# A four-layer graph network in groups of eight graphs: the stages of a group put beside other groups' stages, roots as powers on GpSimd

## The chip, the cores and the metric

The kernel runs on one core of one Trainium2 chip. A core has five engines that run side by side, each with a queue of its own that it works off in order: TensorE (PE: matrix products, and PEld for its weight loads), VectorE (DVE), ScalarE (ACT), GpSimd (POOL) and SyncE (SP, which here issues DMAs). Data lies in SBUF (128 partitions) and in PSUM, where products land. ACT evaluates functions from tables; a set of functions has to be loaded before one of them can run.

The metric is the device time of one execution in microseconds (us). Times of single instructions come from one profiled execution.

## The reference

128 graphs of 64 nodes with 128 features and a 64x64 adjacency pass four layers. Every layer is `x = x + layer(relu(layernorm(x)), adj)`; only the parts that the change touches are written out.

```
# layer 0: over each edge (i, j), with e = adj[i, j]
g  = exp(coeff * (e - offsets)**2)                  # 64 gaussians
Wf = ssp(g @ W1.T + b1) @ W2.T + b2                 # ssp(x) = softplus(x) - log 2
y  = sum_j (h @ Wa.T)[j] * Wf[i, j] * e * e
x  = x + ssp(y @ Wd1.T + bd1) @ Wd2.T + bd2
# layer 1: hyperbolic attention
h  = proj(mobius_add(proj(mobius_matvec(W, h)), hyp_bias))   # norms, artanh, tanh
att[i, j] = sigmoid(silu(logmap(h_i, h_j) @ att_w1.T + att_b1) @ att_w2.T + att_b2)
s  = mlp(x_self, sum_j att * logmap(h_i, h_j) * adj) + x_self
o  = proj(expmap(s, h))                              # norm, tanh
x  = x + proj(expmap0(silu(logmap0(o))))             # norm, artanh, norm, tanh
# layer 2
x  = x + (D^-1/2 adj D^-1/2 h) @ W + b
# layer 3: deg = adj.sum over senders
m  = where(deg > 0, (adj.T @ (h @ Ws)) / max(deg, 1) + h @ Wr, 0)
x  = x + concat(h, m) @ W_upd
```

## The kernel before

`sparse_stack` works on 16 groups of 8 graphs; a tile of 128 partitions holds two graphs, and a group is four such pairs (`NP = 4`), so most tiles are 128x512. The kernel sorts each graph's nodes by degree and packs the edges of a row into slots: 12 items for a group, 8 of 512 slots and 4 of 275. (`dense_stack`, for inputs that don't fit the slots, isn't run.)

A group g passes five stages, each a Python generator that emits instructions and yields between steps:

- `order(g)` (L1144): sorts nodes, permutes x and adj, builds the slot masks `oh`, the first layer norm and `rf`. 9 steps.
- `layer0(g)` (L1228): for each item a spread of adj over nodes (L1260), Square and Exp, products with W1 and rf (L1275, L1277), Exp, copy and Ln on ACT, a product with W2 (L1286), and on DVE the multiplication and gather (L1288, L1113). At its end (L1334 to L1353) the gathered sums `ys` pass two small products with Exp and Ln between, and give `x1`. 56 steps.
- `layer1_nodes(g)` (L1380): what layer 1 needs for each node and pair of nodes: norms, artanh, tanh, Gram matrices, the tables `U`, `Sx`, `qn`, `mp`, `pq`. 26 steps.
- `layer1_edges(g)` (L1517), the slots of layer 1: for each item products (L1538, L1553, L1556), Silu on ACT, a product to scores (L1564), Tanh on ACT, and on DVE masking and gather. 55 steps.
- `rest(g)` (L1618): end of layer 1, layers 2 and 3, the store. 39 steps. It is a chain of short operations on tiles of one group.

The order of ACT's instructions is the order in which the program emits them (`manual_schedule`, L1798); PE's, DVE's and POOL's queues are ordered by a planner that looks at costs and dependences. `together` (L770) emits several stages in proportion to their steps; `abreast` (L783) takes a step of each in turn. The main loop (L1805 to L1812) runs two stretches for a group g, one after the other: `layer1_edges(g)` with `order(g + 2)`, then `layer0(g + 2)` with `rest(g)` and `layer1_nodes(g + 1)`.

The helper `act` (L999) puts a table load on ACT where the function asked for is in another set than the last: Exp and Ln are in one set, Silu and Tanh in another; Square, Copy and Relu need no load. Roots are Ln and then Exp with a factor (`root`, L1089; `moments`, L1053), so `rest`, which also has Silu and Tanh, changes sets several times, and it changes them for layer 0 too, whose Exp and Ln stand between in ACT's queue. `artanh_ratio` (L1077) is two Ln on ACT and a series on DVE.

POOL has three operations for a group: L1342, L1645, L1729, additions over 128x512. PSUM is full: three buffers `big` of two banks, one `sm`, one `sl`. The wide tiles of `rest` (d0 to d3) and of `layer1_nodes` (b0 to b3) are separate.

Of the kernel before, what the change touches and what calls it, by code (L numbers as in the profile page):

```python
# [11 lines left out]
F32 = mybir.dt.float32  # L12
# [8 lines left out]
NP = 4  # L21
# [744 lines left out]
STEPS0, STEPS1, ORDER, NODES1, REST = 56, 55, 9, 26, 39  # L766
# [3 lines left out]
def together(*gens):  # L770

    gens = [(g, n) for g, n in gens if g is not None]
    most = max(n for _, n in gens)
    for i in range(most):
        for g, n in gens:
            for _ in range((i + 1) * n // most - i * n // most):
                next(g, None)
    for g, _ in gens:
        for _ in g:
            pass  # L780
# [12 lines left out]
def sparse_stack(ctx: ExitStack, tc: tile.TileContext, ins, out: bass.AP, flag):  # L793
# [34 lines left out]
    epsc = const.tile([P, 1], F32, name="epsc")  # L828
    G.memset(epsc, EPS_LN)
# [49 lines left out]
    def weight_t(ap, name, dst=None):  # L879
# [3 lines left out]
        if dst is None:  # L883
# [72 lines left out]
    wmsg = const.tile([P, 2 * P], F32, name="wmsg")  # L956
    nc.sync.dma_start(out=wmsg.rearrange("d (s u) -> d s u", s=2),
                      in_=ins["L3_gnn_W_msg"].rearrange("(s d) u -> d s u", s=2))
    wupd = const.tile([P, 2, P], F32, name="wupd")
    nc.sync.dma_start(out=wupd, in_=ins["L3_gnn_W_upd"].rearrange("(s d) u -> d s u", s=2))  # L960

# [6 lines left out]
    state = {"evac": S, "set": None}  # L968
    HALF = [slice(0, N), slice(N, P)]

    def evac(dst, src):

        if state["evac"] is S:
            S.copy(dst, src)
        else:
            V.tensor_copy(dst, src)
# [75 lines left out]

    def moments(x):  # L1053

        raw, mv = ttile("ln_raw", NP, 6), ttile("ln_mv", NP, 2)
        bn(mv, raw, x)
        yield
        rstd = ttile("ln_r")
        act(AF.Ln, rstd, mv[:, :, 1], bias=epsc)
        act(AF.Exp, rstd, rstd, scale=-0.5)  # L1060
        return mv, rstd

# [26 lines left out]
    def root(n):  # L1089

        act(AF.Ln, n, n)
        act(AF.Exp, n, n, scale=0.5)
# [43 lines left out]
    def load(g):  # L1136
        x = pers.tile([P, NP, D], F32, name="x", tag="x")
        adj = pers.tile([P, NP, N], F32, name="adj", tag="adj", bufs=4)
        gs = slice(2 * NP * g, 2 * NP * (g + 1))
        nc.sync.dma_start(out=adj, in_=adj_d[gs].rearrange("(p b) i j -> (b i) p j", b=2))  # L1140
        nc.sync.dma_start(out=x, in_=x_d[gs].rearrange("(p b) i d -> (b i) p d", b=2))
        return {"x": x, "adj": adj}

    def order(g, st):  # L1144
# [19 lines left out]
        xp = st["xp"] = wtile("xp")  # L1164
# [10 lines left out]
        adjT = st["adjT"] = etile("adjT", 3)  # L1175
        raw, mv = ttile("ln_raw", NP, 6), tiny.tile([P, NP, 2], F32, name="mv0", tag="mv0")
        bn(mv, raw, xp)
        st["mv"] = mv
# [9 lines left out]
        V.tensor_tensor(h, xp, bl(mv[:, :, 0], D), ALU.subtract)  # L1188
        yield
        oh = st["oh"] = pers.tile([P, NP, SLOTS + SLOTS % 2], BF, name="oh", tag="oh", bufs=3)  # L1190
        for c in range(3):
# [9 lines left out]
            elif c == 1:  # L1201
                act(AF.Relu, hT, pt)
                pt = pairs_mm(hT, lambda p: waT)
            else:
                st["rf"] = wtile("a2")
                evac(st["rf"], pt)
# [21 lines left out]
    def layer0(st):  # L1228

        xp, oh, adjT, rf = st["xp"], st["oh"], st["adjT"], st["rf"]  # L1230
        sr = ttile("sr")
        act(AF.Ln, sr, st["mv"][:, :, 1], bias=epsc)
        act(AF.Exp, sr, sr, scale=-0.25)
        ys = [wtile(f"y{c}") for c in range(2)]
# [71 lines left out]
        for t in range(n + 1):  # L1306
# [20 lines left out]
            if t % 2 == 0:  # L1327
                if t + 2 < n:
                    squares((t + 2) // 2)
                if t + 4 < n:  # L1330
# [3 lines left out]
        spn = wtile("a0")  # L1334
        pt = big()
        pre, x1p = pt[:, 0, :], pt[:, 1, :]
        T.matmul(pre, lhsT=wd1T, rhs=flat(ys[0]), start=True, stop=False)
        T.matmul(pre, lhsT=wd1T, rhs=flat(ys[1]), start=False, stop=False)
        T.matmul(pre.rearrange("q (x r) -> q x r", r=N)[:, :, 0:RC], lhsT=wd1T, rhs=ys[2],
                 start=False, stop=True)  # L1340
        xb = wtile("a2")
        G.tensor_tensor(xb, xp, bm(bd2s, NP), ALU.add)  # L1342
        yield
        ex = wtile("a1")
        act(AF.Exp, flat(ex), pre, bias=bd1)
        V.tensor_scalar(ex, ex, EXP_MAX, None, ALU.min)
        act(AF.Ln, ex, ex, bias=1.0)
        V.scalar_tensor_tensor(flat(spn), pre, bd1, flat(ex), ALU.add, ALU.max)
        x1 = st["x1"] = pers.tile([P, NP, D], F32, name="x1", tag="x1", bufs=3)
        for p in range(NP):  # L1350
            T.matmul(x1p[:, D * p:D * p + D], lhsT=spn[:, p, :], rhs=wd2T, start=True, stop=True)
        V.tensor_tensor(flat(x1), x1p, flat(xb), ALU.add)
        yield  # L1353

# [14 lines left out]
    def proj_scale(v, tmp, hn, sc):  # L1369

        act(AF.Square, tmp, v)
        reduce_d(hn, tmp)
        V.tensor_scalar(hn, hn, MIN_NORM2, None, ALU.max)
        yield
        root(hn)
        V.reciprocal(sc, hn)
        V.tensor_scalar(sc, sc, MAXNORM, 1.0, ALU.mult, ALU.min)
        yield

    def layer1_nodes(st):  # L1380

        x1 = st["x1"]
        mv, rstd = yield from moments(x1)
        h1, tmp, hT = wtile("b0"), wtile("b1"), wtile("b2")
# [10 lines left out]
        mx = wtile("b3")  # L1395
# [7 lines left out]
        nn = ttile("nn", 2, NP)  # L1403
        V.tensor_scalar(nn, n2, MIN_NORM2, None, ALU.max)
        yield
        root(nn)
# [3 lines left out]
        yield  # L1410
        artanh_ratio(r, s)
        rr, arg = ttile("rr", 2, NP), ttile("arg")
        V.reciprocal(rr, nn)
        V.tensor_tensor(arg, r, s, ALU.mult)
        V.tensor_tensor(arg, arg, rr[:, 0], ALU.mult)
        V.tensor_tensor(arg, arg, mxn, ALU.mult)
        yield
        yield
        t = ttile("t")
        act(AF.Tanh, t, arg)  # L1420
# [8 lines left out]
        yield  # L1429
# [5 lines left out]
        yield from proj_scale(mx, tmp, hn, sc)  # L1435
# [81 lines left out]
    def layer1_edges(st):  # L1517
# [100 lines left out]
    def rest(g, st):  # L1618
# [8 lines left out]
        supT, xsT = wtile("d1"), wtile("d2")  # L1627
# [13 lines left out]
        hid = wtile("d0")  # L1641
# [7 lines left out]
        u, tmp, tmp2 = wtile("d3"), wtile("d1"), wtile("d2")  # L1649
# [3 lines left out]
        un2, un, uh, k_ = ttile("un2"), ttile("un"), ttile("uh"), ttile("k_")  # L1653
        act(AF.Square, tmp, u)
        V.tensor_tensor(tmp2, u, hh, ALU.mult)
        reduce_d(uh, tmp2)
        reduce_d(un2, tmp)
        V.tensor_scalar(un, un2, MIN_NORM2, None, ALU.max)
        rb = ttile("rb")
        V.tensor_scalar(rb, st["beta"], 1e-15, None, ALU.max)  # L1660
        V.reciprocal(rb, rb)
        yield
        root(un)
        V.tensor_tensor(rb, rb, un, ALU.mult)
        V.reciprocal(un, un)
# [3 lines left out]
        V.tensor_tensor(k_, k_, un, ALU.mult)  # L1669
# [7 lines left out]
        scaled(tmp, hh, ca)  # L1677
        scaled(u, u, cc)
        V.tensor_tensor(u, u, tmp, ALU.add)
        yield  # L1680
        hn, sc = ttile("d_hn"), ttile("d_sc")
        yield from proj_scale(u, tmp, hn, sc)

        s, r = ttile("d_s"), ttile("d_r")
        V.tensor_tensor(s, hn, sc, ALU.mult)
        V.tensor_scalar(s, s, ATMAX, 1e-15, ALU.min, ALU.max)
        yield
        artanh_ratio(r, s)
        V.tensor_tensor(r, r, sc, ALU.mult)
        scaled(u, u, r)  # L1690
        yield
        yield
        act(AF.Silu, u, u)
        act(AF.Square, tmp, u)
        reduce_d(un2, tmp)
        V.tensor_scalar(un, un2, MIN_NORM2, None, ALU.max)
        yield
        yield
        root(un)
# [3 lines left out]
        V.reciprocal(un, un)  # L1703
        V.tensor_tensor(k_, k_, un, ALU.mult)
        x2 = wtile("x2")
        scaled(u, u, k_)
        V.tensor_tensor(x2, u, x1, ALU.add)
        yield
# [9 lines left out]
        mv, rstd = yield from moments(x2)  # L1718
        act(AF.Ln, dn, dn)
        act(AF.Exp, dn, dn, scale=-0.5)  # L1720
        V.tensor_tensor(rstd, rstd, dn, ALU.mult)
        hs = wtile("d2")
        normed(hs, x2, mv, rstd)
        yield
        sT = wtile("d0")
# [5 lines left out]
        x3r = wtile("d3")  # L1731
        V.tensor_tensor(x3r, pairs_mm(sT, lambda p: w2g), bl(dn, D), ALU.mult)
        V.tensor_tensor(x3r, x3r, x2, ALU.add)
# [21 lines left out]
        V.tensor_scalar(ind, deg, 0.0, None, ALU.is_gt)  # L1755
        V.tensor_scalar(rdeg, deg, 1.0, None, ALU.max)
        V.reciprocal(rdeg, rdeg)
        V.tensor_tensor(rdeg, rdeg, ind, ALU.mult)
        mv, rstd = yield from moments(x3)
        h3, h3T = wtile("d2"), wtile("d1")  # L1760
        normed(h3, x3, mv, rstd)
        yield
        pt = transposes(h3)
# [3 lines left out]
        xs, xr = wtile("d0"), wtile("d3")  # L1767
        for q in range(NP // 2):
            pt = bank(2 * P)
            for k in range(2):  # L1770
                T.matmul(pt[:, k, :], lhsT=h3T[:, 2 * q + k, :], rhs=wmsg, start=True, stop=True)  # L1771
            yield
            two = slice(2 * q, 2 * q + 2)
            evac(xs[:, two, :], pt[:, :, 0:P])
            V.tensor_tensor(xr[:, two, :], pt[:, :, P:2 * P], bl(ind[:, two], D), ALU.mult)
        yield
        msg, msgT, y = wtile("d2"), wtile("x2"), wtile("d3")
        pt = bank()
        graphs_mm(pt, adj, xs)
        V.tensor_tensor(msg, pt, bl(rdeg, D), ALU.mult)  # L1780
# [68 lines left out]
```

## Time and profile before

| | us |
|---|---|
| median of 3 runs | 2774.13 (2764.31 to 2775.21) |
| the profiled execution | 2772.69 |
| its span, first to last instruction | 2770.9 |
| PE busy | 2244.2 (81%) |
| DVE busy | 2041.9 (74%) |
| ACT busy | 1714.9 (62%) |
| of it table loads, 189 of 1.283 us | 242.5 |
| POOL busy | 111.1 (4%) |
| mean granted clock of PE, share of full speed | 0.876 |

Times in the profile are from the span's start. A row of the windows view gives a stretch, its length, and for each engine its busy time and instructions in it, the granted clock of PE, the share of DMA and GB/s. A row of the timeline gives start, duration, engine, line, operation and tiles, and in brackets how long the engine had been idle and what ended that. A row of the groups by line gives a count, then the busy time of the group and the mean duration of one in ns, then idle time before them. Helpers give their own line to all their callers: L1009 is every function on ACT, L974 every copy out of PSUM on ACT, L1113 every gather, L1107 every spread, L1003 and L1007 the table loads. The chain that ended last is 46% PE, 36% ACT and 15% DVE of the span.

### The profile page before, as it was taken

The page shows a single profiled execution, that of the slowest core. Times are in us where ns is not written, and L with a number is a line of the kernel's source. Part 1 is how long each engine was busy: PE and PEld are TensorE (multiplying, and loading weights), DVE is VectorE, ACT ScalarE, POOL GpSimd, SP SyncE. Part 2 cuts the span into 40 slices and gives each one's busy share as a digit, 9 for nine tenths or more (in the row PEclk, how much of TensorE's full clock was granted, in tenths as well). Part 3 has the DMA queues.
Part 4 walks back from the last instruction along what each step waited for, and adds up shares of the span by engine and source line. Part 5 has one row for each costly group of instructions (what it writes and reads, how often), then busy time and mean ns, then how long its engine had stood idle before and what let it go on. Part 6 is the DMA issues. An engine that isn't in the chain of part 4 may idle for free.

```text
span 2770.9 us, 28227 instructions
## 1 busy us (share of the span) xinstructions
PE 2244.2 (81%) x9841; PEld 1067.9 (39%) x9841; DVE 2041.9 (74%) x4741; ACT 1714.9 (62%) x2769; POOL 111.1 (4%) x72
## 2 busy tenths in 40 slices
PE   5889797887979888797988979788797987979483
PEld 2433343434434343343434434343343434434232
DVE  4587877877777777877777787777877777776653
ACT  3676848476584856749375673846749376583432
POOL 0000000000000000000000000000000000000000
PEclk9889899998989989898898988989899898988585
DMA  1000000000000000000000000000000000000000
GB/s 38 4 4 1 0 10 0 10 1 2 8 1 10 1 6 4 1 10 1 10 1 6 5 1 10 0 6 4 1 10 0 7 0 1 5 0 4 1 4 6
DMA packets 29498, 13.72 MB, mean 5 GB/s; under 512 B 10528, under 2 KB 29344, under 8 KB 29344
## 3 DMA queue, kind: packets, MB, share of 16 engines
q1 hardware_dynamic: 29344, 11.80, 1.6%
q8 instruction: 80, 1.31, 0.2%
q14 instruction: 74, 0.61, 0.1%
HBM read 7.61 MB, written 4.19 MB: 4 GB/s over the span
## 4 chain that ended last, share of the span: by engine, by line
PE 46%; ACT 36%; DVE 15%; issue 2%; DMA 0%; SPq 0%; DVEq 0%; ACTq 0%
ACT ex L1009 8%; PE big L1553 6%; PE big L1286 6%; PE sl L1564 6%; PE big L1538 6%; ACT e L1009 5%; PE big L1556 5%; ACT L1003 4%; ACT L1007 3%; ACT va L1009 3%; ACT ra L1009 3%; PE sm L1029 3%; PE sl L1260 2%; PE sm L1771 2%; DVE ex L1288 2%
## 5 line engine op out<-in xcount | busy, mean ns | idle before, releaser
L1286 PE MATMUL big<-ex,w2T 128*128 128x512 f32 (+1 forms) x768 | 420.1, 680 | 104.3 <-ACT ex L1009 103.2
L1009 ACT ACTIVATE ex<-big,c_L_gnn_att_b 128x1024 f32<-128x1024 f32 (+1 forms) x192 | 188.5, 982 | 327.3 <-PE big L1556 327.3
L1260 PE MATMUL sl<-va,bones 128*128 128x512 f32 (+1 forms) x384 | 211.4, 637 | 94.6 <-ACT e L1009 75.3
L1288 DVE SCALAR_TENSOR_TENSOR ex<-big,c_L_gnn_b,ra 128x1024 f32<-128x1024 f32 x128 | 163.9, 1281 | 160.9 <-PE big L1286 145.4
L1286 PEld LDWEIGHTS big<-ex,w2T 128*128 128x128 f32 x768 | 163.4, 233 | 285.1 <-ACT ex L1009 160.4
L1275 PE MATMUL big<-e,w1T 64*128 64x512 f32 (+1 forms) x768 | 224.2, 621 | 59.9 <-ACT e L1009 43.0
L1277 PE MATMUL big<-va,a 64*128 64x512 f32 (+1 forms) x768 | 213.6, 578 | 27.0 <-ACT ex L1009 22.5
L1553 PE MATMUL big<-va,U 64*128 64x512 f32 (+1 forms) x768 | 216.4, 571 | 0.0
L1009 ACT ACTIVATE ex<-big,c_L_gnn_b 128x1024 f32<-128x1024 f32 (+1 forms) x192 | 186.2, 970 | 34.9 <-PE big L1275 34.5
L1564 PE MATMUL sl<-ex,aw2b 128*64 128x512 f32 (+1 forms) x768 | 191.3, 552 | 9.2 <-ACT th L1009 9.1
L1556 PE MATMUL big<-slot_r,Sx 64*128 64x512 f32 (+1 forms) x768 | 195.5, 525 | 0.0
L1009 ACT ACTIVATE ex<-ex 128x1024 f32<-128x1024 f32 (+1 forms) x192 | 177.2, 923 | 0.3
L1576 DVE SCALAR_TENSOR_TENSOR th<-th,oh 128x1024 f32<-128x1024 f32 (+1 forms) x80 | 99.2, 1240 | 102.0 <-ACT th L1009 101.5
L1538 PE MATMUL big<-va,bones 128*128 128x512 f32 (+1 forms) x384 | 166.6, 556 | 7.8 <-DVE va L1107 7.7
L1009 ACT ACTIVATE ra<-big 128x1024 f32<-128x1024 f32 (+1 forms) x192 | 170.0, 885 | 0.7 <-PE big L1277 0.5
L1113 DVE TENSOR_REDUCE y<-ex 128x128 f32<-128x1024 f32 x128 | 154.8, 1209 | 1.4
L1009 ACT ACTIVATE th<-sl,hab 128x512 f32<-128x512 f32 (+1 forms) x192 | 118.7, 618 | 59.3 <-PE sl L1564 35.3
L1260 PEld LDWEIGHTS sl<-va,bones 128*128 128x128 f32 x384 | 78.2, 222 | 187.4 <-ACT e L1009 118.9
L1544 DVE COPY_PREDICATED va<-slot_r,big 128x1024 f32<-128x1024 uint32 (+1 forms) x96 | 108.5, 1130 | 42.1 <-PE big L1538 41.8
L1275 PEld LDWEIGHTS big<-e,w1T 64*128 64x128 f32 x768 | 68.2, 202 | 169.3 <-ACT e L1009 60.2
L1009 ACT ACTIVATE e<-sl,noff 128x512 f32<-128x512 f32 (+1 forms) x192 | 117.6, 612 | 20.9 <-PE sl L1260 20.9
L1277 PEld LDWEIGHTS big<-va,a 64*128 64x128 f32 x768 | 83.9, 205 | 116.3 <-issue 46.9
(501 smaller groups left out, 4051.2 us busy)
## 6 DMA issues: line engine op xcount, KB each, us to landing
x<-in_x_dram SPq DMA_DIRECT2D x16, 256.0 KB, 2.8
out_dram<-d SPq DMA_DIRECT2D x16, 256.0 KB, 2.2
adj<-in_adj_dram SPq DMA_DIRECT2D x16, 128.0 KB, 2.2
raw<-in_L_gnn_mlp_w_dram SPq DMA_DIRECT2D x3, 64.0 KB, 1.8
wmsg<-in_L_gnn_W_msg_dram SPq DMA_DIRECT2D x1, 128.0 KB, 5.6
wupd<-in_L_gnn_W_upd_dram SPq DMA_DIRECT2D x1, 128.0 KB, 5.6
raw<-in_L_gnn_Wd_dram SPq DMA_DIRECT2D x2, 64.0 KB, 3.7
raw<-in_L_gnn_W_dram SPq DMA_DIRECT2D x2, 64.0 KB, 1.7
```

What stands on the lines that cost most here:

```text
L1003: S.preload_act_table_set("natural_log_exp_and_others")
L1009: S.activation(*args[:2], func, **kw)
L1113: V.tensor_reduce(dst[:, :, r0:r0 + n], part(a, at, k, n), AX.X, ALU.add)
L1260: T.matmul(spreads[i][:, 0:W], lhsT=bones, rhs=weights[h][:, own(h).start + i % 2, :], start=True, stop=True)
L1275: T.matmul(pre[:, b, 0:W], lhsT=w1T[rows, :], rhs=e[rows, 0:W], start=True, stop=True)
L1277: T.matmul(nb[:, b, 0:W], lhsT=rf[rows, p, :], rhs=factors[h][rows, own(h).start + i % 2, :], start=True, stop=True)
L1286: T.matmul(wf[:, b, 0:W], lhsT=w2T, rhs=ex[:, b, 0:W], start=True, stop=True)
L1288: V.scalar_tensor_tensor(ex, wf, b2s, ra, ALU.add, ALU.mult)
L1538: T.matmul(rows_[h][:, k, 0:W], lhsT=bones, rhs=firsts[h][:, own(h).start + k, :], start=True, stop=True)
L1553: T.matmul(pre[:, b, 0:W], lhsT=U[rows, p, :], rhs=coefs[h][rows, own(h).start + i % 2, :], start=True, stop=False)
L1556: T.matmul(pre[:, b, 0:W], lhsT=Sx[rows, p, :], rhs=slot_r[rows, at:at + W], start=False, stop=True)
L1564: T.matmul(pas[i][rows, 0:W], lhsT=aw2b, rhs=a[:, b, 0:W], start=True, stop=True)
```

## The change

The stages are put beside others. Each iteration `it` now has, in units of a planned time line of 99.2 for an iteration: `layer1_edges(it)` at 0 to 54 with `rest(it - 1)` at 3.4 to 50.4; `layer0(it + 2)` at 51.6 to 104.6, so past the end of the iteration, with `layer1_nodes(it + 1)` and `order(it + 3)` abreast at 53.4 to 97.4; the load of group `it + 4` at 60. `weave` sorts all steps by that time and emits them. So Silu and Tanh fall into the first stretch and Exp and Ln into the second.

For that, `rest` has no Exp or Ln left and `layer1_nodes` no Tanh: every root and reciprocal there is a power on POOL (`power`, a tensor_tensor with a constant tile of exponents); the artanh of `rest` is halved by three square roots and a series, all on POOL (`artanh_halved`); the tanh of `layer1_nodes` is a power of e squared and a series on POOL (`tanh_power`). Some DVE work of `rest` goes to ACT: squares with their sums (`squares_sum`), the normalization with Relu (`normed_act`), both in four pieces of 128 columns with a scale or sum for each pair. DVE's multiply and add become one instruction in four pieces (`plus_scaled`). The end of layer 0 moves to the head of `layer1_nodes`, so it stands beside the next group's layer 0. Layer 3's message weights are multiplied with the update weights once, in the setup (`wsu`, `wru`): the transposition of the messages and one product per group go. `rest` and `layer1_nodes` share the wide tiles w0 to w3; adj has five buffers, xp three, adjT four, rf two.

```diff
+def weave(*gens):
+    events = []
+    for k, (g, n, first, last) in enumerate(gens):
+        events += [(first + i * (last - first) / (n - 1), k, g) for i in range(n)]
+        events.append((last + 0.01, k, None))
+    for _, k, g in sorted(events, key=lambda e: e[:2]):
+        for _ in gens[k][0] if g is None else [next(g, None)]:
+            pass
...
+    for k, dst in enumerate((wsu, wru)):
...
+        T.matmul(ps[:, :P], lhsT=rawT, rhs=wupd[:, 1, :], start=True, stop=True)
...
+    def power(dst, src, e):
...
+        G.tensor_tensor(dst, src, exps[e][:, 0:n], ALU.pow)
     def moments(x):
...
-        act(AF.Ln, rstd, mv[:, :, 1], bias=epsc)
-        act(AF.Exp, rstd, rstd, scale=-0.5)
+        G.tensor_scalar(rstd, mv[:, :, 1], EPS_LN, None, ALU.add)
+        power(rstd, rstd, -0.5)
...
+    def normed_act(dst, x, mv, r):
+        shift = ttile("ln_s")
+        V.scalar_tensor_tensor(shift, mv[:, :, 0], -1.0, r, ALU.mult, ALU.mult)
+        for p in range(NP):
+            act(AF.Relu, dst[:, p, :], x[:, p, :], bias=shift[:, p:p + 1], scale=r[:, p:p + 1])
+    def squares_sum(dst, tmp, x):
+        for p in range(NP):
+            act(AF.Square, tmp[:, p, :], x[:, p, :], accum_out=dst[:, p:p + 1])
+    def plus_scaled(dst, a, col, b):
+        for p in range(NP):
+            V.scalar_tensor_tensor(dst[:, p, :], a[:, p, :], col[:, p:p + 1], b[:, p, :],
+                                   ALU.mult, ALU.add)
...
+    def artanh_halved(r, s):
+        c, d, q, w = (ttile(f"ah{k}") for k in range(4))
+        G.tensor_scalar(c, s, -1.0, 1.0, ALU.mult, ALU.add)
+        pool_stt(d, s, 1.0, c, ALU.add, ALU.mult)
+        power(c, d, 0.5)
...
+        for k in range(2):
+            pool_stt(c, c, 2.0, w, ALU.mult, ALU.mult)
+            power(c, c, 0.5)
...
+        for k in (11, 9, 7, 5, 3):
+            pool_stt(q, q, 1.0 / k, w, ALU.add, ALU.mult)
...
+    def tanh_power(t, a):
+        e, z, q = (ttile(f"tp{k}") for k in range(3))
+        G.tensor_scalar(e, a, 20.0, None, ALU.min)
+        G.tensor_tensor(e, exps[E2][:, 0:NP], e, ALU.pow)
+        G.tensor_scalar(e, e, 1.0, None, ALU.add)
+        power(e, e, -1.0)
...
     def rest(g, st):
...
+        squares_sum(hn, tmp, u)
+        proj_scale(hn, sc)
+        G.tensor_tensor(s, hn, sc, ALU.mult)
+        G.tensor_scalar(s, s, MAXNORM, 1e-15, ALU.min, ALU.max)
+        artanh_halved(r, s)
+        G.tensor_tensor(r, r, sc, ALU.mult)
+        for _ in range(7):
+            yield
+        for p in range(NP):
+            act(AF.Silu, u[:, p, :], u[:, p, :], scale=r[:, p:p + 1])
...
-            two = g + 2 < GROUPS
-            together((layer1_edges(sts[g]), STEPS1), (order(g + 2, sts[g + 2]) if two else None, ORDER))
-            together((layer0(sts[g + 2]) if two else None, STEPS0),
-                     (abreast(rest(g, sts[g]),
-                              layer1_nodes(sts[g + 1]) if g + 1 < GROUPS else iter(())), REST))
+        for it in range(-2, GROUPS + 1):
+            begin = it * 99.2
...
+                streams.append((of(layer1_edges, it), EDGES, begin, begin + EDGES - 1))
...
+                streams.append((of(rest, it - 1), REST, begin + 3.4, begin + 50.4))
...
+                streams.append((of(layer0, it + 2), LAYER0, begin + 51.6, begin + 50.6 + LAYER0))
+            streams.append((nodes(it), NODES, begin + 53.4, begin + 97.4))
+        weave(*streams)
```

The new step counts are `EDGES, LAYER0, NODES, REST = 55, 54, 28, 41`. `proj_scale` is a maximum, two powers and one more step on POOL; `pool_stt` is two POOL steps.

## The prediction

> **What bounds the kernel now.** I read first the start of each stage (first product of each group's layer 1 slots, L1553, and of its layer 0, L1275), then the busy time by stage, then ACT's order of time, then the last group's `rest`, which runs alone. Slots start at 211.1 us for group 0 and at 2358.3 for group 13: 165.2 us for a group. Of that 50 us pass from the first slot product to layer 0's first (1191.1 to 1242.1) and 113 us from there to the next slots (1355.2). The stages by engine:
>
> ```profile
> core 0: us, PE busy (x) PEld busy (x) DVE busy (x) ACT busy (x) POOL busy (x), PEclk, DMA share, GB/s
> 1022.00:1066.00 44.00, 43.48 (x215) 18.56 (x214) 32.49 (x62) 19.01 (x24) 0.00 (x0) 1.00 0.04 13
> ...
> 1073.60:1152.30 78.70, 58.53 (x216) 24.39 (x216) 60.42 (x167) 71.50 (x117) 3.25 (x2) 0.91 0.00 1
> 1152.30:1186.00 33.70, 28.20 (x149) 18.54 (x149) 26.42 (x56) 12.33 (x26) 3.69 (x1) 0.80 0.02 5
> ```
>
> The slots are PE's (43.5 of 44 us). Then come 79 us in which ACT is busy 91%: layer 0, `rest` and `layer1_nodes` in one queue. Then 34 us that no engine fills: layer 0's narrow items wait for the end of `rest`, a chain of short steps. ACT's queue in the second stretch:
>
> ```profile
> 1106.54 1.28 ACT L1007 ACT_TABLE_LOAD   x1
> 1107.84 0.20 ACT L1009 ACTIVATE t<-arg 128x4 f32<-128x4 f32 x1
> 1108.06 1.28 ACT L1003 ACT_TABLE_LOAD   x1
> 1109.35 1.11 ACT L1009 ACTIVATE ex<-big,c_L_gnn_b 128x1024 f32<-128x1024 f32 x1
> 1110.48 1.28 ACT L1007 ACT_TABLE_LOAD   x1
> 1111.78 0.20 ACT L1009 ACTIVATE k__7231<-rb 128x4 f32<-128x4 f32 x1
> ```
>
> Two 0.2 us Tanh cost three loads. The reader should note that the next ACTIVATE starts 0.01 to 0.02 us after a load, so one costs 1.3 us. The groups by line count 95 (L1003) and 94 (L1007).
>
> The best pattern for the new second stage is already there: layer 0 of group 1 with `layer1_nodes` of group 0 and no `rest`. And `rest` of group 15 runs alone at the end:
>
> ```profile
> 129.60:190.30 60.70, 55.28 (x207) 24.86 (x206) 42.30 (x92) 58.49 (x96) 1.28 (x1) 0.93 0.00 1
> 190.30:211.10 20.80, 12.78 (x44) 6.00 (x44) 20.55 (x39) 3.02 (x5) 0.00 (x0) 0.75 0.04 13
> ```
>
> ```profile
> 2640.00:2690.00 50.00, 46.06 (x213) 19.30 (x212) 29.40 (x42) 21.25 (x29) 1.26 (x1) 1.00 0.02 6
> 2690.00:2771.00 81.00, 31.03 (x154) 21.72 (x154) 28.34 (x95) 19.10 (x35) 1.26 (x1) 0.53 0.02 5
> ```
>
> **Table loads.** By the act() rule the new order leaves a load where slots start and one where layer 0 starts: 32 instead of 189. 157 x 1.30 = 204 us of ACT, 13 per group, nearly all inside the ACT-bound 79 us. [...]
>
> **Second stage: layer 0, nodes, order.** ACT: the 60.7 us stretch, less its two loads (2.6, of which one comes back), plus `order` (2.5 by its rows L974 and L1009) and layer 0's end, now the head of `layer1_nodes` (0.69 + 0.63): about 63. DVE by rows: layer 0 32.5 (L1288, L1113, L1107, L1293), `order` 10.7 (half of it L1195), nodes 26.2 with 1.2 for the moved end: 70.6. PE: 93.1 us in 1066 to 1186, less `rest` (23.3, the sum of its rows over 16), plus `order` (6.2): 76 at the clock of 0.89, 68 at full clock. The nodes chain took 57 us in that stretch (133.6 to 190.7); layer 0's end adds 7 in front (its Exp to its x1, 196.4 to 201.5, and some 2 of products before), POOL's powers about 12 (below): 76, less two loads, 74. The head also holds one of three `big` buffers through two of its steps while layer 0 wants three per item; that is within the 7. After the last nodes' Ln stood 20.8 us of DVE work in which PE sat half idle; half of it (layer 0's end, 4.5 us of slots) now lies beside other work, and layer 0's last items stand behind it in ACT's queue as cover. I take 76 for the stage: the chain's 74, DVE's 70.6 under it, 2 of hand-over. Bounds: 68 (DVE just not full, chain hidden) and 88 (74, and at each of its some 35 changes of engine half of the 0.7 us that a 512-column operation of ACT or DVE takes, as a wait).
>
> **First stage: slots and `rest`.** PE: slots alone 46 us at full clock (above); `rest` 31.0 at 0.53, so 16.4 at full clock, less what goes: L1771 (54.8), L1791 (25.7), half of L1015 on `d` (13.9) for two sets of 128-wide products (25.0 each, as L1022 w2g): 44 us in all, 2.8 per group. Sum 60; by the rows without the clock's help 66. ACT 19.2 + 14 and DVE 32.2 + 15.2 (`scaled`, reduces and roots leave DVE; pieces of 128 cost some 0.3 each by the line through 0.16 for 4, 0.42 for 256 and 0.69 for 512 columns) fill less. But the chain of `rest` must pass too. Alone it takes 2687.1 to 2760.7, 73.6 us. At full clock its 31 us of PE halve: 59. Four loads stood on it (1.1, 0.4, 0.4 and 1.3 us: 3.2) and the message transposes (2752.8 to 2756.2: 3.4): 52. POOL then adds about 17: 69. With the wait for the first Silu, 71.
>
> **POOL.** The trace has no power on POOL and no chained 4-column operation. Its rows:
>
> ```profile
> L829 POOL MEMSET epsc<- 128x1 f32 x1 | 0.1, 98 | 0.0
> ```
>
> ```profile
> 1149.51 1.26 POOL L1729 TENSOR_TENSOR x<-x,r_L_gnn_b 128x512 f32<-128x512 f32 x1 [73.10 <-DVE d L1065]
> 1171.87 3.69 POOL L1342 TENSOR_TENSOR a<-xp,r_L_gnn_bd 128x512 f32<-128x512 f32 x1 [21.10 <-PE big L1277]
> ```
>
> ```profile
> 1170.94 1.22 DVE L1107 TENSOR_TENSOR va<-oh,qn 128x1024 f32<-128x1024 bf16 x1
> 1172.07 1.22 DVE L1107 TENSOR_TENSOR va<-oh,pq 128x1024 f32<-128x1024 bf16 x1
> 1173.21 1.22 DVE L1107 TENSOR_TENSOR va<-oh,qn 128x1024 f32<-128x1024 bf16 x1
> ```
>
> A dependent 4-column step on DVE comes every 0.20 us; POOL's 512-column add takes 1.26 against DVE's 0.69, so a plain step on POOL is 0.2 to 0.37, I take 0.25. A power lies between 0.10 (the memset) and 1.26; it is more work per element than an add, so I take 0.9, near the upper end. From u's squares to its Silu are 41 chained steps, 8 of them powers: 33 x 0.25 + 8 x 0.9 = 15.5 us, where now 4 pass (2713.8 to 2717.8): +11.5. The two norms, two moments and one degree that change from Ln and Exp (0.44) to plain step and power add about 1 each: 17 in all. Cover: the new ACT order puts two Silu and three Tanh of slots between; seven steps of the 55 at 71 us are about 9 us. So ACT stands some 6 us with slot Silus behind it, PE fills its `big` buffers and then waits; it costs this because PE's 60 us cannot be made up in less than the chain. In nodes: tanh_power (20 steps, 2 powers: 18 x 0.25 + 2 x 0.9) 6.3 for a Tanh with its load 1.5, three roots 2 to 3 more each: 12. Ends of the unknown: all at 0.1, chain 52 + 1, the stage is PE's 60; powers at 1.26 and steps at 0.37, 26 instead of 17: 80.
>
> L1342 took 3.69 where L1729 took 1.26: it began behind three DVE operations and ended 1.26 after the last. [...]
>
> **What hides the rest.** Loads of x and adj move one group earlier on SP (fifth adj buffer); they land in 2.8 us against 147. Behind each in SP's queue is only the output of `rest` or the next load. `rest` and nodes now share w0 to w3: the nodes' hT waits for y's store (2.2 us), hidden by the nodes' first five steps; uncovered, 2 us per group, 30 in all. Setup gains two transposes and products; SP already waits on `raw` there (to 26.5 us): 0 to 8, I take 4.
>
> **The sum.** The execution shown is 2772.7 us with a span of 2770.9; the median is 2774.1, 1.4 more, which I neglect. Slots of group 0 start at 211.1; less about 23 (order 1 and layer 0's two ends no longer stand alone: 190.3 to 211.1 halves, 100 to 125 loses half), plus 4: 192. Fourteen groups at 71 + 76 = 147, without `rest` in the first (24): 2226. Then slots and `rest` 71, nodes of group 15 without layer 0 75, slots and `rest` 71, `rest` alone 86 (81 - 6 + 11): **2529**. A us per group is worth 15.5; no gain is at 163.
>
> **Rivals.**
> - POOL is cheap (below 0.2 a step, 0.4 a power): PE's 60 and 68, 2529 - 15.5 x 19 = 2235 if all else is ideal, some 2330 with two thirds of it. For it: the short slots of POOL's memsets. Against: the chain's DVE steps remain. Chance 0.10.
> - DVE and the hop waits set both stages: 75 and 82, 2684. For it: 70.6 us of DVE in the second stage and one of three `big` buffers held at its start. Against: ACT ran at 96% in the 60.7 us. Chance 0.20, still faster.
> - [...] Of 70 steps on the two chains at 0.38 now (15.5/41), each 0.1 more is 7 us per group; 16 us per group more, at 0.61, is no gain, and at 0.75 it is 26 x 15.5 = 400 us more: 2930. ACT, in order, would then stand before Silu u and hold every slot behind it. For it: 3.69 against 1.26. [...] Chance 0.14.
> - The stage split does nothing because the chains, not the loads, set the stages: same within 0.5%, 0.03. (0.5% is about what a measurement here can tell from none.)
>
> My forecast, 2529, has 0.53. Its own bounds, 2400 to 2660, come from 60 to 80 and 68 to 84. The range for 8 in 10 is 2380 to 2740. Faster by over 0.5%: 0.53 + 0.10 + 0.20 = 0.83; same 0.03; slower 0.14.
>
> **What would show it.** 34 table loads with setup's two. From first slot product to layer 0's first about 71 us, then 76. POOL busy 20 to 35 us per group, powers near 0.9 us. ACT's longest waits before Silu on `w` released by POOL, about 6 us a group. Clock above 0.9. It is wrong if powers cost over 1.3 us, if DVE passes 95% of the second stage, or if slots' PE falls below 80% for another reason than Silu u.

## The result, and the profile after

The changed kernel takes 3153.3 us (2774.7 before): a ratio of 1.137, with a 95% interval of 1.135 to 1.140. The prediction had 2529.

The busy line and the line of engines in the chain that ended last, on the page of the changed kernel:

```profile
PE 2271.0 (72%) x9783; PEld 1057.7 (34%) x9783; DVE 1895.0 (60%) x4233; ACT 1538.1 (49%) x2852; POOL 770.7 (24%) x1484
...
DVE 32%; PE 26%; POOL 19%; ACT 16%; issue 6%; DMA 1%; SPq 0%; DVEq 0%; ACTq 0%; POOLq 0%
```

ACT lost 177 us of work and DVE 147, PE gained 27 and GpSimd 660, and yet the span grew by 381. No engine is near full: PE, the busiest, is at 72%. GpSimd, absent from the chain before, holds 19% of it; ACT's share fell from 36% to 16%. The work of no single engine explains the longer span, so the time went into waiting. The table loads left, by the groups by line:

```profile
L1009 ACT ACT_TABLE_LOAD x16 | 20.5, 1283 | 0.3
L1013 ACT ACT_TABLE_LOAD x16 | 20.5, 1283 | 0.3
```

These are 32 for 189 (the program has two more, in the setup). The two stages of one cycle, in the windows view (columns as before: PE, PEld, DVE, ACT, POOL busy, clock; the first begins 1 us after the first slot product):

```profile
1299.40:1392.30 92.90, 66.62 (x320) 31.17 (x316) 44.30 (x105) 36.30 (x83) 29.06 (x58) 0.85 0.00 1
1392.30:1487.40 95.10, 71.95 (x292) 32.72 (x294) 72.81 (x158) 59.44 (x96) 19.27 (x33) 0.89 0.03 7
```

Slots with `rest` take 93 us where 71 were forecast, and layer 0 with the nodes and `order` 95 where 76 were. The work in them is about what was forecast: PE 67 and 72, DVE 44 and 73, ACT 36 and 59. So the stages are longer than the work of any engine by 22 to 26 us. What fills the difference is seen in the first stage, by following one group's `rest` from step to step. Beside the slots of the next group (timeline of the changed kernel, seven marks of the chain; start, duration, instruction, and in brackets the idle time before it):

```profile
1305.14 0.41 DVE L1703 TENSOR_TENSOR r<-sm,ident 128x256 f32<-128x256 f32 x1
...
1315.44 0.69 DVE L1720 TENSOR_TENSOR w<-sm,xself 128x512 f32<-128x512 f32 x1
...
1326.67 1.28 ACT L1015 ACTIVATE w<-hh,d_ca 128x128 f32<-128x128 f32 x4 [5.64 <-DVE d_cc L1419]
...
1330.20 0.23 POOL L1423 TENSOR_SCALAR d_hn<-d_hn 128x4 f32<-128x4 f32 x1 [10.18 <-ACT w L1015]
...
1350.01 1.28 ACT L1015 ACTIVATE w<-w,d_r 128x128 f32<-128x128 f32 x4 [11.83 <-POOL d_r L1759]
...
1379.04 1.65 ACT L1015 ACTIVATE w<-x,ln_s,ln_r 128x128 f32<-128x128 f32 x4 [5.21 <-DVE ln_s L1078]
...
1391.19 1.11 DVE L1090 SCALAR_TENSOR_TENSOR w<-sm,rdeg,w 128x128 f32<-128x128 f32 x4
```

The same seven marks of the last group, whose `rest` runs alone (timeline of the changed kernel, later stretch):

```profile
3062.17 0.43 DVE L1703 TENSOR_TENSOR r<-sm,ident 128x256 f32<-128x256 f32 x1 [1.04 <-PE sm L1702]
...
3072.41 0.69 DVE L1720 TENSOR_TENSOR w<-sm,xself 128x512 f32<-128x512 f32 x1 [8.89 <-PE sm L1028]
...
3080.27 1.28 ACT L1015 ACTIVATE w<-hh,d_ca 128x128 f32<-128x128 f32 x4 [1.83 <-DVE d_cc L1419]
...
3082.80 0.23 POOL L1423 TENSOR_SCALAR d_hn<-d_hn 128x4 f32<-128x4 f32 x1 [4.80 <-ACT w L1015]
...
3101.00 1.28 ACT L1015 ACTIVATE w<-w,d_r 128x128 f32<-128x128 f32 x4 [18.28 <-POOL d_r L1759]
...
3126.85 1.65 ACT L1015 ACTIVATE w<-x,ln_s,ln_r 128x128 f32<-128x128 f32 x4 [5.01 <-DVE ln_s L1078]
...
3140.71 1.13 DVE L1090 SCALAR_TENSOR_TENSOR w<-sm,rdeg,w 128x128 f32<-128x128 f32 x4 [1.28 <-PE sm L1035]
```

Take the differences of the starts, mark to mark: 10.3, 11.2, 3.5, 19.8, 29.0, 12.2 beside the slots; 10.2, 7.9, 2.5, 18.2, 25.9, 13.9 alone. The sums are 86.1 and 78.5. The chain is no shorter beside the slots, although PE's clock is 0.84 there (1305 to 1391) against 0.50 alone (3058 to 3142): steps queue behind slot work, and that takes more than the clock gives. And 86 of the stage's 93 us are this one chain.

### The profile page after: what moved, and what is told of

The parts are those of the page before. It is cut to its first block, busy times and chain, and to the rows that moved or that the text cites. A ratio compares the mean times of both kernels' runs of the same rounds, so it can differ in the third digit from the quotient of the medians.

```text
span 3151.7 us, 29213 instructions
## 1 busy us (share of the span) xinstructions
PE 2271.0 (72%) x9783; PEld 1057.7 (34%) x9783; DVE 1895.0 (60%) x4233; ACT 1538.1 (49%) x2852; POOL 770.7 (24%) x1484
## 4 chain that ended last, share of the span: by engine, by line
DVE 32%; PE 26%; POOL 19%; ACT 16%; issue 6%; DMA 1%; SPq 0%; DVEq 0%; ACTq 0%; POOLq 0%
ACT w L1015 5%; DVE va L1180 5%; ACT ex L1015 4%; PE sm L1028 4%; DVE y L1186 3%; POOL ah L1064 3%; DVE ex L1361 3%; PE big L1359 3%; DVE va L1614 2%; PE big L1623 2%; PE big L1626 2%; PE sl L1634 2%; PE big L1348 2%; DVE oh L1271 2%; ACT e L1015 2%
## 5 line engine op out<-in xcount | busy, mean ns | idle before, releaser
L1634 PE MATMUL sl<-ex,aw2b 128*64 128x512 f32 (+1 forms) x768 | 246.7, 659 | 253.7 <-ACT th L1015 251.2
L1359 PE MATMUL big<-ex,w2T 128*128 128x512 f32 (+1 forms) x768 | 329.8, 549 | 19.3 <-ACT ex L1015 6.3
L1348 PE MATMUL big<-e,w1T 64*128 64x512 f32 (+1 forms) x768 | 240.2, 632 | 64.1 <-ACT ex L1015 47.6
L1608 PE MATMUL big<-va,bones 128*128 128x512 f32 (+1 forms) x384 | 206.2, 670 | 99.0 <-DVE va L1180 98.3
L1646 DVE SCALAR_TENSOR_TENSOR th<-th,oh 128x1024 f32<-128x1024 f32 (+1 forms) x80 | 108.1, 1351 | 254.5 <-ACT th L1015 254.5
L1015 ACT ACTIVATE w<-w 128x128 f32<-128x128 f32 (+1 forms) x256 | 96.7, 379 | 302.5 <-DVE w L1498 186.1
L1350 PE MATMUL big<-va,rf 64*128 64x512 f32 (+1 forms) x768 | 231.8, 592 | 5.1 <-ACT ex L1015 5.0
L1626 PE MATMUL big<-slot_r,Sx 64*128 64x512 f32 (+1 forms) x768 | 204.5, 557 | 0.0
L1361 DVE SCALAR_TENSOR_TENSOR ex<-big,c_L_gnn_b,ra 128x1024 f32<-128x1024 f32 x128 | 163.7, 1279 | 67.5 <-PE big L1359 64.9
L1359 PEld LDWEIGHTS big<-ex,w2T 128*128 128x128 f32 x768 | 131.7, 191 | 169.4 <-issue 87.0
L1634 PEld LDWEIGHTS sl<-ex,aw2b 128*64 128x64 f32 x768 | 48.8, 154 | 359.6 <-ACT th L1015 282.7
L1608 PEld LDWEIGHTS big<-va,bones 128*128 128x128 f32 x384 | 83.2, 237 | 218.3 <-issue 175.1
L1186 DVE TENSOR_REDUCE y<-ex 128x128 f32<-128x1024 f32 x128 | 155.2, 1212 | 0.7
L1614 DVE COPY_PREDICATED va<-slot_r,big 128x1024 f32<-128x1024 uint32 (+1 forms) x96 | 107.3, 1118 | 59.0 <-PE big L1608 59.0
```

Of the source, the lines that this page charges most:

```text
L1015: S.activation(*args[:2], func, **kw)
L1186: V.tensor_reduce(dst[:, :, r0:r0 + n], part(a, at, k, n), AX.X, ALU.add)
L1348: T.matmul(pre[:, b, 0:W], lhsT=w1T[rows, :], rhs=e[rows, 0:W], start=True, stop=True)
L1350: T.matmul(nb[:, b, 0:W], lhsT=rf[rows, p, :], rhs=factors[h][rows, own(h).start + i % 2, :], start=True, stop=True)
L1359: T.matmul(wf[:, b, 0:W], lhsT=w2T, rhs=ex[:, b, 0:W], start=True, stop=True)
L1361: V.scalar_tensor_tensor(ex, wf, b2s, ra, ALU.add, ALU.mult)
```

## The experiments

For every run the mean cycle of some of the middle groups is split at the first slot product and at layer 0's first product, as in the prediction (another choice of groups moves a figure by up to 0.5 us):

| run | time, us | cycle | slots to layer 0 | layer 0 to slots |
|---|---|---|---|---|
| before | 2774.7 | 166.2 | 51.7 | 114.5 |
| changed kernel | 3153.3 | 188.8 | 94.6 | 94.1 |
| artanh left out | 2968.9 | 177.6 | 83.4 | 94.2 |
| tanh left out | 3047.9 | 182.6 | 94.9 | 87.7 |
| new bodies, old order | 2817.0 | 165.5 | 51.5 | 114.0 |
| old bodies, new order | 2886.1 | 173.1 | 90.7 | 82.5 |
| second Silu later | 3160.2 | 189.7 | 95.5 | 94.1 |
| nodes off GpSimd | 2994.0 | 179.4 | 95.1 | 84.3 |
| `rest` cut at x2, artanh on GpSimd | 2788.3 | 163.9 | 79.8 | 84.0 |
| the same, artanh as Ln | 2554.9 | 148.4 | 64.2 | 84.3 |
| short chains, `rest` whole | 2803.0 | 167.3 | 83.0 | 84.2 |

All but the two kernels of the change and the version with `rest` cut and artanh as Ln are single times, beside single times of the kernel before of 2766.8 and 2772.9, or its median of 2766.9. Two theories stood at the start. A: the long chains of short steps set the stages, and ACT, in order, stands before their next instruction. B: something else sets them (the hand-over between stages, DVE, GpSimd steps held up beside DVE's operations), and the waits only show where there is room.

**Each long GpSimd chain left out.**

```diff
     def artanh_halved(r, s):
-        c, d, q, w = (ttile(f"ah{k}") for k in range(4))
...
+        G.tensor_scalar(r, s, 1.0, None, ALU.mult)
```

> The changed kernel with the artanh of `rest` left out: its 31 chained GpSimd instructions are one, and the factor before the second Silu is wrong. Theory A (ScalarE stands in order before that Silu, 11.8 us a group in the profile, with all slot Silus behind it, and nothing takes the wait's place): the cycle loses 11 to 15 us, 2915 to 2985 us. Theory B (the stage's length is set elsewhere, by the hand-over between stages and by PE and DVE; the wait only moves to the next ScalarE instruction): less than 4 us a group, over 3090.

Measured 2968.9, in A's range: the first stage lost 11.2 us, the second nothing. (The trace has 34 instructions in the artanh, not 31.)

```diff
     def tanh_power(t, a):
-        e, z, q = (ttile(f"tp{k}") for k in range(3))
...
+        G.tensor_scalar(t, a, 1.0, None, ALU.mult)
```

> The changed kernel with the tanh of `layer1_nodes` left out: 20 GpSimd instructions are one. Theory A (the nodes' chain sets the second stage, ScalarE stood 11.7 us in it): the cycle loses 7 to 11 us, 2975 to 3040 us. Theory B (DVE, 72.8 us busy of 95.1, and the hand-over set it): less than 3 us a group, over 3105.

Measured 3047.9: the second stage lost 6.4 us of a chain of 6.8, the cycle 6.2, just outside A's range and far from B's. Each chain lengthens its own stage, and only that stage: the tanh by nearly its whole length, the artanh by 11 of its 16 us.

**The two halves of the change, apart.** The old order with the new bodies has `together` and the loop of before:

```diff
-        weave(*streams)
+            together((layer1_edges(g, sts[g]), EDGES), (order(g + 2, sts[g + 2]) if two else None, ORDER))
+            together((layer0(g + 2, sts[g + 2]) if two else None, LAYER0),
+                     (abreast(rest(g, sts[g]),
+                              layer1_nodes(g + 1, sts[g + 1]) if g + 1 < GROUPS else iter(())), REST))
```

> The new bodies of `rest` and `layer1_nodes` (powers on GpSimd, squares with sums, folded message weights) in the old order of stages: `rest` beside layer 0 and the nodes, `order` beside the slots, layer 0's end in layer 0. 150 table loads instead of 191. If the stage split costs the time and the powers are covered: 2650 to 2790 us. If the GpSimd chains cost it wherever they stand: over 2900.

Measured 2817.0, a little over the range, and it is worth seeing why: the cycle is 165.5, the same as before. Of the 44 us 39 are at the ends, where chains run alone: the first slots come at 228.2 instead of 211.1, and from the last slots to the end pass 149 instead of 127. In the old order the GpSimd chains lengthen the cycle by nothing, and the 41 loads saved shorten it by nothing. That both are covered fits this; that one offsets the other isn't ruled out.

The kernel before with `weave`, the new loop and layer 0's end in `layer1_nodes`, but every root as Ln and Exp:

```diff
-            together((layer1_edges(sts[g]), STEPS1), (order(g + 2, sts[g + 2]) if two else None, ORDER))
...
+            if 0 <= it - 1 < GROUPS:
+                streams.append((of(rest, it - 1), REST, begin + 3.4, begin + 50.4))
...
+        weave(*streams)
```

> The old bodies (every root Ln and Exp, artanh and tanh on ScalarE) in the new order of stages; 281 table loads instead of 34 (247 x 1.28 = 316 us more of ScalarE, 20 a group, beside a ScalarE busy 96 of 188 us). If the GpSimd chains cost the time: 2700 to 2900 us, since artanh and tanh take some 15 us less a group. If the split costs it whatever the roots are: over 3050.

Measured 2886.1, in the first case, near its upper end. With 247 table loads more than the changed kernel it is 267 us faster than it. So neither half alone is the loss: the new bodies cost 44 us, the new order 113, both together 379. The GpSimd chains cost what they do because the new order has taken their cover away. But the first stage is 90.7 us without them too: here the chain of `rest` takes 78 to 81 us beside the slots, from the row `r<-sm,ident` to the store, and 67.5 alone.

**Only the place in ACT's order.** If the wait before the second Silu hurts because slot work stands behind it, this Silu should be put later:

```diff
-        for _ in range(7):
+        for _ in range(16):
             yield
         for p in range(NP):
             act(AF.Silu, u[:, p, :], u[:, p, :], scale=r[:, p:p + 1])
```

> The changed kernel; 16 steps instead of 7 stand between the GpSimd artanh and the second Silu of `rest` in ScalarE's order, so more slot Silus and Tanhs come first (the other steps of `rest` stand 18% closer). If the wait costs because slot work stands behind it in the queue: the 11.8 us before this Silu fall to 4 or less and the cycle loses 5 us or more, under 3080 us. If the chain of `rest` is itself the length of the first stage, wherever its Silu stands: 3110 to 3200 us, and the wait is found before other instructions.

Measured 3160.2: the second case. The waits view of the changed kernel (waiting instruction, what it waited for, us in total, times, longest):

```profile
ACT w L1015 <- POOL d_r L1759: 186.6, 16, 18.3
...
ACT x L982 <- PE sm L1035: 61.5, 16, 7.2
```

and of this run:

```profile
ACT x L982 <- PE sm L1035: 148.6, 16, 10.9
...
ACT w L1015 <- POOL d_r L1759: 135.2, 16, 18.3
```

The wait for the artanh fell from 11.2 us a group (186.6 less the 18.3 of the last one, over 15) to 7.8, not to 4, and a later wait of the same chain, for the permuted x3, rose by 87 us in total, more than the 51 that were saved. This parts A in two: the stage did not follow the place of this Silu on ACT, as it would if that set it, but stayed as long as the chain. The prediction's wording ("ACT stands some 6 us with slot Silus behind it") named the place where it shows, not what sets it.

**The nodes off GpSimd.** In the second stage Ln and Exp cost no load (the run with short chains, further down, has such nodes and 64 loads, four a group: two for the stages and two for its artanh), so the roots go back to them, and a tanh can be made of an Exp:

```diff
-        tanh_power(t, arg)
+        yield from tanh_exp(t, arg)
...
+        act(AF.Exp, e, e, scale=2.0)
+        V.tensor_scalar(e, e, 1.0, None, ALU.add)
+        V.reciprocal(e, e)
+        V.tensor_scalar(e, e, -2.0, 1.0, ALU.mult, ALU.add)
+        V.copy_predicated(t, z.bitcast(U32), e)
```

> The changed kernel with `layer1_nodes` off GpSimd: its roots are Ln and Exp again, its tanh an Exp on ScalarE (the same table set) and five short DVE steps. First stage as it is. If the nodes' chain sets the second stage: 95 becomes 82 to 87 us (leaving the tanh out gave 6.4, the roots are another 5), 2950 to 3030 us. If DVE and the hand-over set it: 90 us or more, over 3070.

Measured 2994.0, in the range for the chain: the second stage fell to 84.3, the first stayed.

**`rest` cut in two.** Only the part to x2 needs Silu and Tanh. The other part (`tail`: layers 2 and 3) can stand beside layer 0, and `order` beside the slots:

```diff
+            if it > -2:
+                streams.append((abreast(of(rest, it - 1), of(order, it + 2)), 26, begin + 3.4, begin + 50.4))
...
+            streams.append((abreast(of(layer1_nodes, it + 1), of(tail, it - 1)), 29, begin + 53.4, begin + 97.4))
```

> `rest` cut at x2: the part with Silu and Tanh stays beside the slots with the GpSimd artanh, and `order` comes back beside them; layers 2 and 3, which use no table set, go beside layer 0 and the nodes, with roots as Ln and Exp there, and the nodes as in the run with the nodes off GpSimd. If the lengths of the two chains set the two stages (rest to x2: 54 us of 82 to 93; nodes with the cheap roots about 65): stages of 62 to 72 and 76 to 86, a cycle of 138 to 158, 2400 to 2700 us. If the waits in ScalarE's order add up whatever the chain's length: a cycle over 165, over 2800 us.

Measured 2788.3, between the two cases: a cycle of 163.9. The second stage is in the range, the first is 79.8, not 62 to 72. The 54 us for the chain to x2 came from a profile without `order` beside it. With it, PE is busy 43 of the first 46 us (1159.1 to 1205.0), and the artanh comes only then, with hardly a slot item left to cover it. The waits view of this run has 15.2 us a group for it (245.9 less 18.3, over 15), where the changed kernel had 11.2:

```profile
ACT w L1017 <- POOL d_r L1798: 245.9, 16, 18.3
```

Then the artanh as well:

```diff
-        artanh_halved(r, s)
-        G.tensor_tensor(r, r, sc, ALU.mult)
+        for _ in range(3):
+            yield
+        artanh_ratio(r, s)
+        V.tensor_tensor(r, r, sc, ALU.mult)
```

> The same with the artanh of `rest` as two Ln on ScalarE and a series on DVE: two table loads a group more (2.6 us of ScalarE), and a chain of some 6 us instead of 15. If the chain still sets the first stage: 5 to 9 us a cycle less than with the GpSimd artanh, 75 to 135 us. If the first stage is PE's or the hand-over's by then: within 40 us of it.

Measured 2555.2, 233 us less, far more than the 75 to 135 expected: 15.6 us a group in the first stage, about the whole of that wait. The ACT rows of its timeline show what stands in the artanh's place:

```profile
1135.85 1.28 ACT L1011 ACT_TABLE_LOAD   x1
1137.21 0.20 ACT L1017 ACTIVATE at_p<-d_s 128x4 f32<-128x4 f32 x1
1137.32 0.19 ACT L1017 ACTIVATE at_m<-d_s 128x4 f32<-128x4 f32 x1
1137.53 1.28 ACT L1015 ACT_TABLE_LOAD   x1
...
1140.74 1.27 ACT L1017 ACTIVATE w<-w,d_r 128x128 f32<-128x128 f32 x4
```

From the load to the Silu pass 4.9 us, and the second load (1137.5 to 1138.8) lies under the DVE series (1137.2 to 1140.0). On GpSimd the same took 16 in the changed kernel (1333.8 to 1349.8). The change had avoided two loads of 1.3 us at the price of a chain three times as long. The windows of one cycle of this version:

```profile
1087.00:1151.10 64.10, 58.67 (x285) 24.03 (x284) 50.10 (x118) 35.15 (x76) 13.09 (x14) 1.00 0.02 5
1151.10:1235.10 84.00, 72.10 (x326) 35.00 (x326) 70.74 (x181) 66.00 (x120) 2.64 (x2) 0.96 0.02 5
```

PE is now busy 92% of the first stage at full clock: a still shorter chain could save 5 us there at most. In the second nobody is full (PE 86%, DVE 84%, ACT 79%).

**Is the cut needed?** `nodes` off GpSimd and the artanh as Ln, with `rest` whole:

> The stage split of the changed kernel, `rest` whole and `order` beside the nodes, but both long GpSimd chains gone: the nodes as in the run with the nodes off GpSimd, the artanh of `rest` as two Ln (two table loads more a group) and a DVE series. If the chains' lengths set the stages: the first stage falls from 95 by 7 to 12 us, the second is the 84 us of that run, a cycle of 167 to 172 us, 2800 to 2880 us, still slower than before, so the split of `rest` is needed as well. If the GpSimd chains were all that was wrong with the new order: under 2700 us.

Measured 2803.0: the chain's length still sets the first stage (83.0; from the row `r<-sm,ident` to the store 76.2, and 67.0 alone), and the kernel is still slower than before. Short chains and the cut together make the gain. The fastest version once more:

> The fastest version so far again (`rest` cut at x2, its artanh as Ln, the nodes off GpSimd), timed in rounds beside the kernel before: 2555 us within 10, a ratio of 0.92 to 0.925. If its one time was luck: over 2600 us.

Measured 2554.9 us (median of four), a ratio to the kernel before of 0.922 (0.919 to 0.925). So stages put beside others with few table loads (69 here, for 191) do pay, 8%, once the chains fit.

## Why the prediction was wrong

**Right: what was counted.** 34 table loads with the setup's two. In the two stages ACT's 36 and 59 us for 33 and 63, DVE's 44 and 73 for 47 and 70.6, PE's 67 and 72 for 60 to 66 and 68 to 76. The prices of GpSimd were near: a power 1.04 us for 0.9, a plain step 0.20 to 0.24 for 0.25, the 41 steps to the second Silu 18.2 us alone for 15.5, the tanh 6.8 for 6.3. (GpSimd's busy time was off: 48 us per group, for 20 to 35.) So the rival "slower" came true in its sign but not by its price: the steps took 0.44 us on average alone and 0.48 beside the slots (19.8 over 41), for 0.38 forecast and 0.61 needed. The rival that had the mechanism, "the chains, not the loads, set the stages", was given a chance of 0.03, and it expected the time to stay the same. One sign of being wrong came: PE fell to 72% in the slots' stage.

**Sums that don't come out.** The 88 us as upper end of the second stage should be 86 (74 and 35 times 0.35), and ACT's 63 there started from the length of the stretch, 60.7, where ACT was busy 58.5. The stages' own ends, 60 and 68 or 80 and 84, give 2235 and 2792 us, not 2400 and 2660. Even so both measured stages, 94.6 and 94.1, lie above their upper ends. In the kernel before, L1342 ended 1.13 us after the last of the three DVE operations, not 1.26.

**GpSimd steps beside DVE's operations.** The timeline shows where they took longer (DVE's and GpSimd's rows, first within the artanh of one group, then in the nodes of another):

```profile
1338.22 1.22 DVE L1646 SCALAR_TENSOR_TENSOR th<-th,oh 128x1024 f32<-128x1024 f32 x1 [2.88 <-ACT th L1015]
1338.70 0.84 POOL L1135 TENSOR_SCALAR ah<-ah 128x4 f32<-128x4 f32 x1
1339.36 1.22 DVE L1180 TENSOR_TENSOR va<-oh,adjT 128x1024 f32<-128x1024 bf16 x1
1339.62 1.86 POOL L1064 TENSOR_TENSOR ah<-ah,exp 128x4 f32<-128x4 f32 x1
1340.49 1.21 DVE L1186 TENSOR_REDUCE att<-th 128x128 f32<-128x1024 f32 x1
...
1419.61 2.28 DVE L1271 TENSOR_TENSOR oh<-pos,slot_k 128x2048 bf16<-128x2048 bf16 x1
1419.78 2.22 POOL L1470 TENSOR_SCALAR rr<-n 128x8 f32<-128x8 f32 x1 [12.75 <-DVE n L1047]
```

The plain step that started inside L1646 took 0.84 us, for 0.23 in the last group, and ended 0.10 us after it. The power that started inside L1180 took 1.86, for 1.04, and ended 0.90 us after it. The step that started inside L1271 took 2.22, where the shortest of its 16 took 0.25, and ended 0.11 us after it. Within the reduction L1186 the next steps took 0.19 and 0.24 as elsewhere. Over the whole trace the 30 GpSimd instructions that started inside L1646 took 0.14 to 0.80 us more than the median of their line, and the 47 inside L1186 at most 0.02. L1646, L1180 and L1271 read two SBUF tiles each; L1361 and L1614, which read one of their inputs from `big` in PSUM, put at most 0.01 us on the 77 that started inside them. But the 0.84 and the 1.86 are all that this did to this artanh: it took 16.0 us beside the slots (1333.8 to 1349.8) and 14.6 alone (3086.2 to 3100.8), 1.4 more; the 41 steps took 1.6 more (19.8 for 18.2). DVE was itself standing for ACT in 10.9 of the 16.0 us.

**The step that failed: "At full clock its 31 us of PE halve: 59".** Without this step the forecast's terms come to 84.0 us for the chain of `rest` alone. In the changed kernel the last group's took 83.9 (3058.0 to 3141.8). That this fits to 0.1 is partly luck, since the two stretches don't begin with the same instruction. From the row `r<-sm,ident` to the last sum it is 67.8 us in the kernel before and 79.7 in the changed one (3062.2 to 3141.8 above), 11.9 more for 10.4 forecast. The kernel before, its last group alone:

```profile
2692.86 0.42 DVE L1633 TENSOR_TENSOR r<-sm,ident 128x256 f32<-128x256 f32 x1 [1.04 <-PE sm L1632]
...
2759.94 0.69 DVE L1792 TENSOR_TENSOR d<-sm,x 128x512 f32<-128x512 f32 x1 [5.75 <-PE sm L1791]
```

So the chain was sized well, and what failed is the next term: the forecast took 14.6 us off for the clock, put queueing on PE, DVE and ACT at nothing, and got 69. Beside the slots PE's steps did get shorter (sixteen products of L1035 took 1.09 us for 1.97). Summed over the trace the products of this chain took 17.7 us for 25.3 alone, 7.6 less and not 14.6. Yet the chain took 87.2 (1305.1 to 1392.3) for 79.7, so waiting put 15 us on it. The stage was 94.6 us, for 71. 23 us for 15 cycles are 350 of the 624 us that were missing.

**The same for the nodes: "the chain's 74, 2 of hand-over".** From the Exp of layer 0's end to the first slot product the nodes took 90.3 us beside layer 0 and `order`, and 67.5 for the last group, alone but for the end of `rest` in the first 4 us:

```profile
1396.20 0.68 ACT L1015 ACTIVATE a<-big,c_L_gnn_bd 128x512 f32<-128x512 f32 x1
...
1486.45 1.13 PE L1623 MATMUL big<-va,U 64*128 64x512 f32 x4 [0.28 <-DVE va L1614]
```

```profile
2900.28 0.69 ACT L1015 ACTIVATE a<-big,c_L_gnn_bd 128x512 f32<-128x512 f32 x1
...
2967.79 1.13 PE L1623 MATMUL big<-va,U 64*128 64x512 f32 x4
```

The 74 counted some 2 us of products before this Exp, so the chain alone was shorter than forecast, and queueing was 23 us, for 2. It lies before and behind the tanh, 11 us each, and not in it. With the nodes off GpSimd the same stretch takes 80.4 us, and 59.8 alone: 10 us of the stage went, most of it the chain's own length, and the queueing stayed at 21. With `order` moved away as well, and layers 2 and 3 in its place, the stage is still 84. Whether it is DVE's queue or the hand-over from engine to engine wasn't separated.

**"ACT stands some 6 us"** was 11.2. The cover of nine us by seven steps was 8.0 (19.8 less 11.83); the 41 steps under it took 19.8 instead of 15.5. **"Clock above 0.9"** was 0.849. **The start**, 214 us for 192, and the end, 184 for 157, hold the same two stages.

The method failed in one place: the chain was given the clock of the busy engine without its queue. One sum would have warned. In the kernel before, `rest` and the nodes lay side by side in one stage of 114 us; the change puts them one after the other. By the forecast's own terms without the clock they are 84 and 74, together 158 of the old cycle's 165, which leaves 7 us for all queueing in both stages. Measured, the stages are 11 and 20 us longer than these two, and the cycle is 189.

## What to carry to other kernels

A chain of short dependent steps is a resource like an engine: add up the chains of a cycle, alone as measured, and add queueing beside busy engines, which here was 10% for `rest` and a third for the nodes. Don't subtract for a faster clock: here it gave 7.6 us, and waiting took 15. A chain moved off its cover cost most of its length here (11 of 16 us, 6.4 of 6.8), and two function table loads of 1.3 us on an engine with room were cheaper than thirty steps of 0.2 to 1.0 us that avoid them. When a stage's waits move but its length does not (the later Silu), stop looking at the order of instructions and cut the chain.

## What the runs showed of the hardware

- A power on GpSimd took 1.04 us for 128x4 and 1.65 for 128x8, plain steps 0.20 to 0.24; a dependent step came about 0.3 us after a plain one and 1.1 us after a power.
- PE's busy time for the same 9783 products was 2271 us at a mean granted clock of 0.849 in the changed kernel, where PE was busy 72% of the span, and 2143 at 0.939 with `rest` cut and the artanh as Ln, where it was busy 84%: 128 us less. The clock was 0.50 where PE was busy 29.5 of 84 us (3058 to 3142 in the changed kernel) and 1.00 where it was busy 58.7 of 64.1 (the first stage of the cut version), but 0.80 where it was busy 28.2 of 33.7 (1152.3 to 1186 in the kernel before); what sets it was not shown.
